# Layer 3's gathered matmuls of a four-layer graph-attention stack, given as two column halves each

## The chip, the cores and the metric

The kernel runs on one core of a Trainium2 chip. A core has TensorE (matmuls, shown as PE, with its weight loads as PEld), VectorE (DVE), ScalarE (ACT), GpSimd (POOL), SyncE (SP, which only issues transfers here) and 16 DMA engines. The metric is the device time of one execution in microseconds; lower is better.

## The reference

Four graph-attention layers over 4096 nodes of 256 features, each followed by a residual sum and a layer norm. The adjacency is the same in every layer: an edge with probability 1/256, and the diagonal. Layer 3, cut to what matters:

```python
h = x @ W                                    # 4096 x 256
Wh1, Wh2 = h @ a[:256], h @ a[256:]
e = leaky_relu(Wh1 + Wh2.T, 0.2)             # 4096 x 4096
att = softmax(where(adj > 0, e, -1e12), axis=1)
neg = -softmax(where(adj > 0, -e, -1e12), axis=1)
out = elu(concatenate([att @ x, neg @ x], axis=1) @ fc_W)
x = layernorm(x + out)
```

Layers 0 and 1 have four heads of 64 features, layer 2 two heads of 128. Layer 3 has two "heads" of 256, the positive and the negative softmax. Everything is float32.

## The kernel before

**Tiles.** The 4096 destination nodes are 32 row tiles of 128. A row tile has edges to only some of the source nodes, so its sources are packed: 13 lists of 128 source nodes, gathered by index from HBM, and the tile's own 128 nodes make 14 positions of 128 nodes (`NP` = 14), handled as two halves of 7 (`HALF`). At each position the values `G` hold, for every source node, 257 columns per head in layer 3: 256 values that were multiplied by the softmax's source factor, and one column that collects the denominator. The values are the projected ones, that is, already multiplied by `fc_W`.

**One half tile in layer 3** (`RowTile.half`, `n == 3`). ACT forms the scores for 7 positions (L690) and two exponentials over all of them (L691, L693); DVE masks both (L692, L694). That gives weights `w[1]` and `w[0]`, each 128 source nodes x 7 positions x 128 destination nodes. TensorE then runs, for head 1 and then head 0, seven matmuls that add into that head's own accumulator, `accs[1]` or `accs[0]`, each one PSUM bank (L727). The weights `w[h][:, k, :]` are the stationary operand (128 rows by 128 columns), and the 257 columns of `G` stream past. `start` is given at position 0 and `stop` at position 13. The very last half tile is done position by position (`last_half`, matmuls at L741). In layer 2 the same line adds both heads into one bank, with 129 columns each; in layers 0 and 1 the operands are swapped (L724).

**Whole rows.** Four of the 32 row tiles of layer 3 (one block, `WHOLE[3] = (7,)`) aren't packed: `whole_rows` runs all 32 source tiles for them, dense, from plain transfers, with matmuls of 128 x 128 weights and 257 streamed columns (L1027). These units are dealt out between the half tiles of the other 28 row tiles by `Layer.whole`: after most half tiles comes one unit of four matmuls.

**Order.** Each engine runs its instructions in the order in which the program gives them (`half_with_whole`): matmuls of a half tile, then the previous tile's finish (`positive`, L1099 and L1102, and `finish`, L1119 to L1127, which read the accumulators), then a unit of the whole rows. POOL issues the gathers for the tiles to come (L647), into 30 buffers that come free as the matmuls that read them end. The accumulators of layer 3 rotate through two pools, for even and odd half-tile steps of a tile's start. SP carries masks, edge terms and plain value tiles.

**Other shapes of TensorE's work** that the prediction speaks of: L278 (layer weights folded with the attention vectors; 128 x 128 weights, 1 to 4 streamed columns), L287 (layer 2's bias term; one column of weights), L557 and L560 (projection; L560 adds a bias with one row of weights), L589 (transposes of 1 to 4 columns) and L757 (transposes of 65 rows).

Of the kernel before, what the change touches and what calls it, by code (L numbers as in the profile page):

```python
# [50 lines left out]
P = 128  # L51
# [22 lines left out]
HALF = NP // 2  # L74
# [531 lines left out]
class RowTile:  # L606
# [25 lines left out]
    def load(self, half):  # L632
        L, m, n = self.layer, self.m, self.layer.n
        prog, nc, sh = L.prog, L.nc, L.shared
        if half == 0:
            self.S = prog.ld.tile([P, H4, P], F32, name="S")
            nc.sync.dma_start(out=self.S[:, :TERMS[n]], in_=sh["e"][n][m].partition_broadcast(P))
            self.mk = prog.ld.tile([P, NP, MC], U8, name="mk")
            nc.sync.dma_start(out=self.mk, in_=sh["maskC"][m])
        else:  # L640
            self.y = L.load_x(m)
        for pos in range(HALF * half, HALF * (half + 1)):
            if pos == FRONT:
                nc.sync.dma_start(out=self.place(pos), in_=sh["v"][n][m * P:(m + 1) * P, :])
                continue
            t = pos - (pos > FRONT)
            nc.gpsimd.indirect_dma_start(  # L647
                out=self.place(pos), out_offset=None, in_=sh["v"][n][:NODES[t], :],
                in_offset=bass.IndirectOffsetOnAxis(ap=sh["idx"][:, m, pos:pos + 1], axis=0))

    def half(self, half):
        L, n, nc = self.layer, self.layer.n, self.layer.nc
        prog, sh, S = L.prog, L.shared, self.S
        H, Wd, V, T, A = HEADS[n], WIDTH[n], VALS[n], TERMS[n], LOGS[n]
        if self.accs is None:
            pool = prog.ptwo[1 if n == 3 and self.step % 2 else 0]
            self.accs = [prog.bank(pool) for _ in range(2 if n == 3 else 1)]
        accs = self.accs
        G = [self.place(half * HALF + k) for k in range(HALF)]
        mh = self.mk[:, half * HALF:(half + 1) * HALF, :]  # L660
        if n < 2:

            if prog.masks is None:
                prog.masks = prog.bank(prog.pmask)
            there = prog.masks[:, half * BANK // 2:half * BANK // 2 + HALF * P // 4].bitcast(I32)
            nc.vector.tensor_scalar(there.rearrange("p (t i) -> p t i", t=HALF),
                                    mh.rearrange("p t i -> p (t i)").bitcast(I32)
                                    .rearrange("p (t i) -> p t i", t=HALF)[:, :, :P // 4], 0, None,
                                    op0=ALU.bitwise_or)
            mh = there.bitcast(U8)  # L670
            mh2 = mh.rearrange("p (o i) -> p o i", o=1).to_broadcast([P, 2, HALF * P])
        else:
            mh = mh[:, :, :P]
        pairs = [prog.wp.tile([P, 2, HALF, P], F32, name="w") for _ in range(H // 2)]
        w = [pair[:, k] for pair in pairs for k in range(2)]
        if n < 2:
            w = [w[1], w[2], w[3], w[0]]
        def masked(pair):

            pair = pair.rearrange("p h t i -> p h (t i)")  # L680
            nc.vector.scalar_tensor_tensor(pair, pair, LEAST, mh2, op0=ALU.max, op1=ALU.mult)  # L681

        def d(k, h):
            return G[k][:, V + T + h:V + T + h + 1]

        if n == 3:
            if half == 1 and self.step == L.count - 1:
                return self.last_half(accs, G, w, mh)
            for k in range(HALF):
                nc.scalar.activation(w[0][:, k, :], S[:, 0, :], AF.Relu, bias=d(k, 0))  # L690
            nc.scalar.activation(w[1], w[0], AF.Exp, scale=-1.0)  # L691
            nc.vector.tensor_tensor(w[1], w[1], mh, op=ALU.mult)  # L692
            self.exps = nc.scalar.activation(w[0], w[0], AF.Exp, bias=sh["shift2"])  # L693
            nc.vector.tensor_tensor(w[0], w[0], mh, op=ALU.mult)  # L694
            heads = (1, 0)
        else:
            for h in range(A, T):
                k = 0
                while k < HALF:
                    pos = half * HALF + k  # L700
                    e = 2 if pos % 2 == 0 and k + 1 < HALF else 1
                    if e == 2:
                        dd = self.slots[pos // 2][:, :2 * ROW[n]].rearrange("p (t c) -> p t c", t=2)
                        nc.vector.tensor_tensor(  # L704
                            w[h][:, k:k + 2, :], S[:, h:h + 1, :].to_broadcast([P, 2, P]),
                            dd[:, :, V + T + h:V + T + h + 1].to_broadcast([P, 2, P]), op=ALU.mult)
                    else:
                        nc.vector.tensor_scalar(w[h][:, k, :], S[:, h, :], d(k, h), None, op0=ALU.mult)
                    k += e
            for h in range(A):  # L710
                for k in range(HALF):
                    nc.scalar.activation(w[h][:, k, :], S[:, h, :], AF.Exp, bias=d(k, h))  # L712
                if n == 2:
                    nc.vector.scalar_tensor_tensor(w[h], w[h], LEAST, mh, op0=ALU.max, op1=ALU.mult)  # L714
                elif h % 2 == 0:
                    masked(pairs[h // 2])
            heads = list(range(A, H)) + list(range(A))
        for h in heads:
            for k in range(HALF):
                pos = half * HALF + k  # L720
                how = dict(start=pos == 0 and (n == 3 or h == heads[0]), stop=pos == NP - 1, skip_group_check=True)
                v = G[k][:, h * Wd:(h + 1) * Wd]
                if n < 2:
                    nc.tensor.matmul(accs[0][:Wd, h * P:(h + 1) * P], v, w[h][:, k, :], **how)  # L724
                else:
                    a = accs[h][:, :Wd] if n == 3 else accs[0][:, h * Wd:(h + 1) * Wd]
                    nc.tensor.matmul(a, w[h][:, k, :], v, **how)  # L727

    def last_half(self, accs, G, w, mh):

        nc, sh, Wd = self.layer.nc, self.layer.shared, WIDTH[3]
        V, T = VALS[3], TERMS[3]
        for k in range(HALF):
            d = G[k][:, V + T:V + T + 1]
            nc.scalar.activation(w[0][:, k, :], self.S[:, 0, :], AF.Relu, bias=d)
            nc.scalar.activation(w[1][:, k, :], w[0][:, k, :], AF.Exp, scale=-1.0)
            nc.vector.tensor_tensor(w[1][:, k, :], w[1][:, k, :], mh[:, k, :], op=ALU.mult)
            nc.scalar.activation(w[0][:, k, :], w[0][:, k, :], AF.Exp, bias=sh["shift2"])
            nc.vector.tensor_tensor(w[0][:, k, :], w[0][:, k, :], mh[:, k, :], op=ALU.mult)
            for h in (1, 0):  # L740
                nc.tensor.matmul(accs[h][:, :Wd], w[h][:, k, :], G[k][:, h * Wd:(h + 1) * Wd],  # L741
                                 start=False, stop=k == HALF - 1, skip_group_check=True)

    def copy(self):

# [19 lines left out]
class Layer:  # L765
# [26 lines left out]
    def load(self, m, half):  # L792
        if m < self.count and (m, half) not in self.loaded:
            self.loaded.add((m, half))
            self.tile(m).load(half)
# [794 lines left out]
```

## Time and profile before

| | us |
|---|---|
| median of 3 runs | 2253.98 |
| lowest and highest run | 2251.62, 2256.02 |
| span of the profiled execution | 2249.3 |
| TensorE matmul busy in it | 2014.0 (90%) |
| TensorE weight load busy | 1834.3 (82%) |
| DVE, ACT, POOL busy | 1786.6 (79%), 1737.9 (77%), 1494.4 (66%) |
| mean granted TensorE clock | 0.966 |
| layer 3's matmuls, first to last | 1757 to 2232 |

The page gives the profiled execution's own time by its span, from the first to the last instruction; the median lies 4.7 us above that span. A group's line gives its source line, engine, operation, what it writes and reads, shapes and count; then busy us and mean ns of one, and the idle time before it with what ended it. Matmuls are pipelined, and one is shown from its start until its result is out, so neighbours overlap: the distance between two starts, not the shown length, is what a matmul costs. A float32 matmul of the program appears as two passes, each with a weight load (LDWEIGHTS) and a matmul. A timeline line gives the start and the length of a run of equal instructions, and their number. The chain of work that ended last follows, back from the last instruction, what each step waited for.

### The profile page before, as it was taken

To read this page: it belongs to the slowest core of one execution; us is meant where nothing else is said; L and a number is where in the kernel's file an instruction comes from. 1 tells how busy PE (TensorE), PEld (TensorE's weight loads), DVE (VectorE), ACT (ScalarE), POOL (GpSimd) and SP (SyncE) were. 2 spreads that over 40 slices of the span, in tenths; PEclk is the share of its full clock that TensorE was granted. 3 is DMA by queue.
4 is the path that set the end of the run, shared out by engine and by line. 5 is a ranking of instruction groups with operands and counts; after the bars stand their busy time and mean duration, and the time that the engine had idled before them with its cause. 6 is when DMAs were issued, how large, how long until landed. Compare 5 with 4: busy or idle time off the path is not lost. (4 is left out here: it accounts for less than half of the span.)

```text
span 2249.3 us, 49137 instructions
## 1 busy us (share of the span) xinstructions
PE 2014.0 (90%) x15689; PEld 1834.3 (82%) x15689; DVE 1786.6 (79%) x5060; ACT 1737.9 (77%) x4989; POOL 1494.4 (66%) x1597
## 2 busy tenths in 40 slices
PE   4878889989999969988899898989999999999995
PEld 2658788878899859988888798989998888788784
DVE  2889899999999959987988886887876566566566
ACT  4778988988789859987888776987876677667664
POOL 2107655656677777777777777777773477777773
PEclk7999999999999989999999999999999999999998
DMA  8879877777566665666665666777777688888884
GB/s 284 258 245 360 272 219 250 254 247 228 146 170 191 174 202 168 182 175 175 173 185 162 172 167 171 226 209 223 223 227 225 200 282 280 249 284 270 262 248 130
DMA packets 250319, 492.99 MB, mean 219 GB/s; under 512 B 44385, under 2 KB 156610, under 8 KB 249666
## 3 DMA queue, kind: packets, MB, share of 16 engines
q0 software_dynamic: 81536, 245.30, 38.3%
q1 hardware_dynamic: 163906, 240.26, 33.3%
q10 hardware_dynamic: 4608, 4.20, 0.5%
q8 instruction: 126, 2.06, 0.4%
q14 instruction: 143, 1.17, 0.2%
HBM read 437.05 MB, written 52.54 MB: 218 GB/s over the span
## 5 line engine op out<-in xcount | busy, mean ns | idle before, releaser
L647 POOL DMA_INDIRECT G<-vals,idx x1456 | 1480.7, 1017 | 715.7 <-issue 221.1
L712 ACT ACTIVATE w<-S,G 128x128 f32<-128x128 f32 x3248 | 1001.6, 390 | 140.6 <-DMA G<-vals,idx 101.6
L724 PE MATMUL bank<-w,G 128*65 128x128 f32 x7168 | 837.8, 276 | 59.7 <-DVE w L681 59.3
L724 PEld LDWEIGHTS bank<-w,G 128*65 128x65 f32 x7168 | 798.7, 140 | 69.9 <-DVE w L681 68.4
L681 DVE SCALAR_TENSOR_TENSOR w<-w,bank 128x1792 f32<-128x1792 f32 x256 | 514.6, 2013 | 13.4 <-ACT w L712 11.2
L727 PE MATMUL bank<-G,w 128*128 128x257 f32 (+1 forms) x2660 | 490.8, 342 | 25.7 <-ACT z L1102 13.6
L727 PEld LDWEIGHTS bank<-G,w 128*128 128x128 f32 x2660 | 431.9, 195 | 73.2 <-ACT z L1102 16.4
L1027 PE MATMUL bank<-vw,pw 128*128 128x129 f32 (+1 forms) x2048 | 298.5, 301 | 3.7 <-issue 2.3
L1027 PEld LDWEIGHTS bank<-vw,pw 128*128 128x128 f32 x2048 | 273.6, 191 | 20.1 <-issue 2.8
L690 ACT ACTIVATE w<-S,G 128x128 f32<-128x128 f32 x385 | 137.8, 393 | 136.8 <-DMA G<-vals,idx 90.0
L440 DVE TENSOR_SCALAR oh<-iota,place 128x256 bf16<-128x256 f16 (+2 forms) x992 | 221.8, 298 | 9.4 <-PE bank L446 9.1
L704 DVE TENSOR_TENSOR w<-S,G 128x256 f32<-128x256 f32 x384 | 151.9, 416 | 69.9 <-DMA G<-vals,idx 66.5
L446 PE MATMUL bank<-mk,oh 128*128 128x132 fp8e4 x2336 | 192.1, 226 | 13.8 <-ACT cm L453 7.0
L557 PE MATMUL bank<-wext,xT 128*128 128x268 f32 (+3 forms) x640 | 176.9, 409 | 16.9 <-ACT xT L548 14.1
L446 PEld LDWEIGHTS <-oh 128*128 128x128 bf16 x2336 | 146.9, 99 | 50.4 <-DVE oh L440 12.7
L385 ACT ACTIVATE mk<-raw 128x1024 uint8<-128x1024 int32 x128 | 130.5, 1051 | 28.0 <-DMA raw<-in_adjB_dram 27.7
L557 PEld LDWEIGHTS bank<-wext,xT 128*128 128x128 f32 x640 | 117.2, 200 | 36.0 <-ACT xT L548 16.9
L1017 DVE SCALAR_TENSOR_TENSOR pw<-pw,mw 128x512 f32<-128x512 f32 x192 | 127.6, 689 | 18.2 <-ACT pw L1016 17.5
L1016 ACT ACTIVATE pw<-Sw,d 128x512 f32<-128x512 f32 x192 | 133.2, 711 | 7.5 <-PE bank L1027 7.0
L714 DVE SCALAR_TENSOR_TENSOR w<-w,mk 128x896 f32<-128x896 f32 x80 | 86.6, 1086 | 41.1 <-ACT w L712 37.9
L1024 DVE TENSOR_TENSOR pw<-pw,mw 128x512 f32<-128x512 f32 x64 | 43.6, 691 | 85.4 <-ACT pw L1023 48.0
L692 DVE TENSOR_TENSOR w<-w,mk 128x896 f32<-128x896 f32 x55 | 60.0, 1091 | 59.5 <-ACT w L691 58.2
(140 smaller groups left out, 1563.3 us busy)
## 6 DMA issues: line engine op xcount, KB each, us to landing
raw<-in_adjB_dram SPq DMA_DIRECT2D x128, 512.0 KB
mk<-maskC SPq DMA_DIRECT2D x112, 231.0 KB
G<-vals,idx POOLq DMA_INDIRECT x1456
S<-edge SPq DMA_DIRECT2D x64, 256.0 KB
vw<-vals SPq DMA_DIRECT2D x96, 129.0 KB
xp<-y SPq DMA_DIRECT2D x96, 128.0 KB
y<-xp SPq DMA_DIRECT2D x96, 128.0 KB
mw<-maskW SPq DMA_DIRECT2D x20, 528.0 KB
```

What stands on the lines that cost most here:

```text
L440: nc.vector.tensor_scalar(oh[:, :n * P], iota[:, :n * P], self.place[:, it, j:j + 1], None, op0=ALU.is_equal)
L446: nc.tensor.matmul(accs[b][:, s * MC:(s + 1) * MC], oh[:, (k - a) * P:(k - a + 1) * P], mk[:, j, it, :].bitcast(FP8), start=touches[b][0] ...
L557: nc.tensor.matmul(pp[:, :c1 - c0], self.xT[:, k, :], wext[:, k, c0:c1], start=(k == 0), stop=(k == KT - 1 and brow is None))
L647: nc.gpsimd.indirect_dma_start(out=self.place(pos), out_offset=None, in_=sh["v"][n][:NODES[t], :], in_offset=bass.IndirectOffsetOnAxis(ap= ...
L681: nc.vector.scalar_tensor_tensor(pair, pair, LEAST, mh2, op0=ALU.max, op1=ALU.mult)
L690: nc.scalar.activation(w[0][:, k, :], S[:, 0, :], AF.Relu, bias=d(k, 0))
L704: nc.vector.tensor_tensor(w[h][:, k:k + 2, :], S[:, h:h + 1, :].to_broadcast([P, 2, P]), dd[:, :, V + T + h:V + T + h + 1].to_broadcast([P ...
L712: nc.scalar.activation(w[h][:, k, :], S[:, h, :], AF.Exp, bias=d(k, h))
L724: nc.tensor.matmul(accs[0][:Wd, h * P:(h + 1) * P], v, w[h][:, k, :], **how)
L727: nc.tensor.matmul(a, w[h][:, k, :], v, **how)
L1016: nc.scalar.activation(p, S[:, h], AF.Exp, bias=d)
L1027: nc.tensor.matmul(accs[it][:, c:c + Wd], p[:, it, :], v[:, c:c + Wd], start=(j == 0 and h == heads[0]), stop=(j == NT - 1), skip_group_ch ...
```

## The change

In layer 3 each gathered matmul is given as two. The first takes the weights of the upper 64 destination nodes and writes accumulator rows 0 to 63, the second those of the lower 64 and rows 64 to 127. Both stream the same 257 columns of `G`. Each thus uses 64 of the array's 128 columns: the first the lower-numbered half, the second the other. `start` and `stop` are given to both. The same is done in `last_half`. Layer 2's matmuls and the whole rows stay as they were.

```diff
                 if n < 2:
                     nc.tensor.matmul(accs[0][:Wd, h * P:(h + 1) * P], v, w[h][:, k, :], **how)
+                elif n == 2:
+                    nc.tensor.matmul(accs[0][:, h * Wd:(h + 1) * Wd], w[h][:, k, :], v, **how)
                 else:
-                    a = accs[h][:, :Wd] if n == 3 else accs[0][:, h * Wd:(h + 1) * Wd]
-                    nc.tensor.matmul(a, w[h][:, k, :], v, **how)
+                    for r in (slice(0, P // 2), slice(P // 2, P)):
+                        nc.tensor.matmul(accs[h][r, :Wd], w[h][:, k, r], v, **how)
...
             for h in (1, 0):
-                nc.tensor.matmul(accs[h][:, :Wd], w[h][:, k, :], G[k][:, h * Wd:(h + 1) * Wd],
-                                 start=False, stop=k == HALF - 1, skip_group_check=True)
+                for r in (slice(0, P // 2), slice(P // 2, P)):
+                    nc.tensor.matmul(accs[h][r, :Wd], w[h][:, k, r], G[k][:, h * Wd:(h + 1) * Wd],
+                                     start=False, stop=k == HALF - 1, skip_group_check=True)
```

## The prediction

> **What bounds the kernel now.** I read the page first (parts 1, 2, 5), then the chain of work that ended last, piece by piece, for layer 3, then the stretches in which TensorE idles, and last the few places where the kernel already leaves the full array.
>
> ```profile
> PE 2014.0 (90%) x15689; PEld 1834.3 (82%) x15689; DVE 1786.6 (79%) x5060; ACT 1737.9 (77%) x4989; POOL 1494.4 (66%) x1597
> PE   4878889989999969988899898989999999999995
> PEclk7999999999999989999999999999999999999998
> ```
>
> TensorE is the busiest engine, fullest in the last quarter. Layer 3's matmuls run from 1757 to 2232 us. Its groups, and the chain there:
>
> ```profile
> L727 PE MATMUL bank<-G,w 128*128 128x257 f32 x1429 | 326.6, 387 | 18.2 <-ACT z L1102 13.6 <-DVE w L692 4.7
> L727 PEld LDWEIGHTS bank<-G,w 128*128 128x128 f32 x1428 | 276.2, 194 | 61.6 <-ACT z L1102 16.4 <-DVE w L692 5.1
> L647 POOL DMA_INDIRECT G<-vals,idx x316 | 324.4, 1026 | 96.3 <-PE bank L727 31.4 <-issue 27.1 <-DMA G<-vals,idx 19.2
> ```
>
> ```profile
> 1774.95 6.07 PE bank L727 x28
> 1781.01 3.47 PE bank L1027 x16
> 1784.48 6.07 PE bank L727 x28
> ```
>
> One f32 matmul of the program is two in the trace, each with its own weight load. A half tile has 7 positions x 2 heads = 14 matmuls, 28 passes; 6.07/28 = 0.2167 us per pass, although a pass is shown 0.39 long (pipelined) and its weight load 0.19. So the load lies wholly beside the previous pass, and what counts is the 257 columns that stream past: the pass itself is the bound. Layer 3's gathered work is 28 tiles x 14 positions x 2 heads = 784 matmuls = 1568 passes = 339.8 us; the whole rows (L1027) are 512 passes = 110.9 us. Together 450.7 of the 475 us. TensorE's reserve is in four stretches:
>
> ```profile
> 1934.00:1948.00 14.00, 8.44 (x24) 5.91 (x24) 10.05 (x34) 12.47 (x32) 10.95 (x11) 0.76 0.84 249
> 2064.00:2101.00 37.00, 34.62 (x159) 29.72 (x158) 22.89 (x67) 24.94 (x54) 28.47 (x29) 1.00 0.85 266
> 2101.00:2126.00 25.00, 21.50 (x86) 18.01 (x85) 16.08 (x49) 16.80 (x35) 19.51 (x19) 0.86 0.81 239
> 2197.00:2222.00 25.00, 17.48 (x70) 14.38 (x69) 20.16 (x76) 18.04 (x46) 17.39 (x18) 0.86 0.74 214
> ```
>
> Columns are the stretch, its length, busy PE, PEld, DVE, ACT, POOL, the granted clock. PE idles 5.6 + 2.4 + 3.5 + 7.5 = 19 us and loses some 10 more to the lower clock after an idle gap. These 29 us are all that a slower TensorE could swallow. Who waits for whom in layer 3 (us in total, times, longest):
>
> ```profile
> ACT w L690 <- DMA G<-vals,idx: 75.8, 79, 6.8
> POOL G L647 <- PE bank L727: 40.8, 111, 7.2
> ```
>
> ACT waits for gathered data, and POOL's gathers wait for buffers that L727 frees; neither is late enough to stop TensorE outside the four stretches.
>
> **The change, part by part.** 784 matmuls become 1568; in the trace 1568 passes and 1568 loads are added. A half has 64 columns of weights but streams the same 257 columns, so nothing in a pass becomes shorter by what is known here. Given one after the other, the halves need twice the time; given at once in two halves of the array, the old time. There is no gain in sight, since the old pass already used every column of the array. No DMA, ACT, DVE or POOL instruction is added or moved.
>
> First unknown, **do the halves stream at once?** The order for one position is upper pass 1, upper pass 2, lower pass 1, lower pass 2. Best case: upper pass 2 runs beside lower pass 1, and lower pass 2 beside the next position's upper pass 1, 0.433 per position as now. Worst case: four passes one after the other, +0.433 x 784 = +339.8 us. No row of this trace has two different tiles of the array at work, so both ends stay.
>
> Second unknown, **the load at each change of half.** In the trace no load ever starts before the matmul ahead of it in the program has started: loads and matmuls strictly alternate, x15689 each. With that order, lower pass 1's load starts when upper pass 2 starts, and lower pass 1 waits for it; so does the next upper pass 1. The price of an exposed load has two rows:
>
> ```profile
> 821.07 0.14 PEld L287 LDWEIGHTS bank<-ablk,bcol 128*1 128x1 f32 x4
> 821.24 0.97 PEld L278 LDWEIGHTS bank<-ablk,nat 128*128 128x128 f32 x8
> 2100.13 0.48 PE L727 MATMUL bank<-G,w 128*128 128x257 f32 x1 [1.32 <-ACT z L1102]
> ```
>
> Eight loads that nothing hides: (0.97 - 0.19)/7 = 0.11 us for 128 columns; and the first pass after an idle gap is shown 0.48 long against 0.38. For 64 columns I take half, 0.055; ends 0 (loaded further ahead) and 0.11. Two changes per position: 784 x 2 x 0.055 = 86 us (0 to 172). I take 86, as the strict alternation is the only row on the order.
>
> The Trainium skill speaks against the change here: "TensorE: Matmul & The Clock Gate" (Part 3, The mechanism) says that a load overlaps a running matmul only where the row groups differ, and both halves use all rows. This trace contradicts it for one full-array tile, where the load starts with the running matmul. Taken literally it would expose all four loads of a position, 784 x 4 x 0.055 = +172 us; the same section's measured stagger of about 4 ns between packed matmuls would make it only 784 x 2 x 0.004 = +6 us.
>
> Third, **the change between array shapes.** Whole rows keep 128 columns, so the PE queue now switches twice per burst; layer 3 has 51 gathered bursts. L287 (one column of weights) and L560 (one row) are the places where the kernel already leaves the full shape:
>
> ```profile
> 820.64 0.41 PEld L278 LDWEIGHTS bank<-ablk,nat 128*128 128x128 f32 x3
> 1048.53 0.70 PE L560 MATMUL bank<-brow,ones 1*128 1x262 f32 x2
> 1049.16 0.26 PEld L757 LDWEIGHTS bank<-ident,aT 65*128 65x128 f32 x3 [0.34 <-issue]
> ```
>
> The third L278 load starts at 820.86 and is through at 820.97; L287's starts at 821.07, 0.10 later, though it waits for nothing. On the way back, L287's fourth matmul starts at about 821.14 (25 ns apart) and the next load at 821.24, 0.10 again. L560 to L757: 1049.16 - 1048.53 = 0.63 for two passes of 0.218, so 0.19 over: 0.11 of exposed load and 0.08 to 0.09 of emptying. L589, also few columns, shows no such gap; but it is a transpose, not a matmul as here. I take L287: in, 0.10 + 0.055; out, 0.10 + 0.11. 51 x 0.155 + 50 x 0.21 = 18.4 us (bounds 0, by L589, and that). Queued behind it are the L1027 matmuls and, through the buffers that they and L727 free, POOL's gathers and ACT's z.
>
> Fourth, **the end of a burst.** The last lower pass has no partner: 51 x (0.217 - 0.055) = 8.3 us (0 if serial, 11.1 if loads are hidden).
>
> Sum: 86 + 18.4 + 8.3 = 113 us. Of the reserve I take off 20 of 29: the idle stretches come from late work on ACT and DVE (ACT waits 75.8 us for gathered data in layer 3), which gains time when TensorE slows; the hand-over of an accumulator through z stays. Net +93. The profiled execution spans 2249.3; the median of the timed runs, 2253.98, lies 4.7 above it, and that margin is kept: 2249.3 + 93 + 4.7 = 2347 us.
>
> **The rivals.**
> *Serial halves:* 339.8 + 18.4 - 25 of reserve = +333, 2587 us. For it: nothing in the trace ever shows two matmuls in parallel. Against: the two halves share no columns and no accumulator rows.
> *Fully parallel, loads ahead of time:* 18.4 + 11.1 plus a stagger of 0 to 0.025 us per change (the closest matmul starts on record, L287), 0 to 39; less 10 of reserve. +19 to +58; I take +25, 2279 us. Against: the strict alternation above.
> *Faster:* the half shape streams its columns quicker than 0.217 per pass. It decides once a position takes under 0.433 - 29.5/784 = 0.396 us. At half the time, 170 us would be freed, but POOL's gathers hold: of its idle time in layer 3 only 41 us wait for L727, so about 2254 - 41 = 2213 us. Against: every f32 row, 128 or 257 columns long, streams at the same rate. For it: no row shows a 64-column tile. The skill's "TensorEngine Tiling (Array Packing)" (Theoretical Speedup) promises up to 2x where a dimension is at most 64, which by itself would lead here; but it compares with an array that stands half empty, and this one is full.
> *No change:* parallel, no emptying (as L589), the reserve swallowing 11.1 us of burst ends: 2254 us.
>
> **How the numbers follow.** Exposed loads 0.35 (the likeliest, 2347), fully parallel 0.27, serial 0.27, faster 0.07, no change 0.04. The range goes from 2264 (parallel with more of the reserve) to 2600 (serial with little of it): it leaves out the last two cases and the edges, under 0.2. The likeliest case alone spans 2300 (load half as dear) to 2440 (0.11 per load, all reserve kept). A difference of 0.2% (4.5 us) is about what can be told from no change: faster 0.07, same 0.04, slower 0.89.
>
> **What the changed profile would show.** The burst in the chain tells it: 56 passes in about 6.6 us if parallel, 14 x 0.544 + 0.16 = 7.8 if loads are exposed, 12.1 if serial, 6.07 or less if I am wrong in sign. The switch shows as a gap of some 0.15 to 0.2 us between L1027's passes and the gathered ones on either side; the four idle stretches shrink; POOL waits longer for the gathered matmuls than 40.8 us; the 128-column passes stay at 0.217. The prediction fails most of all if different column halves do, or don't, overlap for f32, which no row here decides.

## The result

The changed kernel takes 2260.17 us (median of 18 runs) against 2252.96 (18 runs); the ratio is 1.003 with a 95% interval of 1.0019 to 1.004, that is 4.3 to 9.0 us slower. The sign was forecast, the size was not: 2347 was predicted, with 2264 as the low end.

From the page of the changed kernel, parts 1, 2 and 5 (the gathered line is now L729, the whole rows L1030, ACT's z L1105):

```profile
PE 2031.3 (90%) x17257; PEld 1759.3 (78%) x17257; DVE 1787.1 (79%) x5060; ACT 1737.3 (77%) x4989; POOL 1495.5 (66%) x1597
PE   4878889989999969989889898999998999999996
PEclk7999999999999979999999998999999999999998
L729 PE MATMUL bank<-G,w 128*64 128x257 f32 x3080 | 351.8, 387 | 9.1 <-ACT z L1105 4.9
L729 PEld LDWEIGHTS bank<-G,w 128*64 128x64 f32 x3080 | 219.3, 139 | 135.2 <-issue 14.8
```

There are twice as many gathered passes (3080 and 56 at the last half tile, against 1568), but their busy time is what it was: 351.8 us here, and 350.9 in the same stretch before. So two passes run side by side. The chain of waits shows it burst by burst, first the changed kernel, then a line of the kernel before, then who waits for whom in the changed kernel:

```profile
1777.15 6.22 PE bank L729 x56
1783.37 3.67 PE bank L1030 x16
1787.03 6.22 PE bank L729 x56
1803.13 1.93 PE bank L1030 x8
```

```profile
1800.08 1.73 PE bank L1027 x8
```

```profile
POOL G L647 <- PE bank L729: 24.8, 54, 8.3
```

56 half passes take 6.22 us; the 28 whole ones took 6.07. Eight whole-row passes take 1.93 instead of 1.73, sixteen 3.67 instead of 3.47. So bursts of either kind became 0.15 to 0.2 us longer; of the 50 gathered bursts of 56 passes, 49 take 6.22 us. POOL's gathers wait less for the gathered matmuls than before (24.8 against 40.8 us), not more as I had written.

Where the 0.15 and 0.2 us lie is seen in the weight loads. TensorE's load timeline, the changed kernel and then the kernel before (start, length, then in brackets the idle time ahead):

```profile
1785.36 1.27 PEld L1030 LDWEIGHTS bank<-vw,pw 128*128 128x128 f32 x6
1786.96 5.83 PEld L729 LDWEIGHTS bank<-G,w 128*64 128x64 f32 x56 [0.33 <-issue]
1793.18 1.38 PEld L1030 LDWEIGHTS bank<-vw,pw 128*128 128x128 f32 x7 [0.39 <-issue]
```

```profile
1783.45 0.62 PEld L1027 LDWEIGHTS bank<-vw,pw 128*128 128x128 f32 x3
1784.10 6.04 PEld L727 LDWEIGHTS bank<-G,w 128*128 128x128 f32 x28
1790.17 1.92 PEld L1027 LDWEIGHTS bank<-vw,pw 128*128 128x128 f32 x9
```

Before, loads follow one another; now an idle 0.33 and 0.39 us stands at the two changes of shape, put down to "issue", a wait for nothing that the profile names. The starts of the matmuls around one such burst, taken from the same trace (us, and distance to the one ahead):

```
1786.654  whole row, last pass
1786.964  half pass   +0.310
1786.970  half pass   +0.006
1787.231  half pass   +0.261
1787.238  half pass   +0.007
1787.448  half pass   +0.210
1787.454  half pass   +0.006
   (and so on, in pairs, 0.217 from pair to pair)
1792.864  half pass   +0.210
1792.871  half pass   +0.007
1793.181  whole row   +0.310
1793.502  whole row   +0.321
1793.719  whole row   +0.217
```

A pass normally starts 0.217 after its predecessor. Going in, the first pair starts 0.310 after the last whole pass and the second pair 0.267 after the first: (0.310 - 0.217) + (0.267 - 0.217) = 0.143 us. I read the first part as the array emptying and the second as a 64-column load that nothing hides. Coming out costs 0.093 plus 0.104, for a 128-column load, 0.197 us. Layer 3 has 51 ways in and 50 out: 17.1 us.

It doesn't all reach the time. The table splits layer 3's stretch, from the first to the last pass of 257 columns, into 2080 pass times of 0.2167 us (a pair counted once), changes of shape at the prices above, idle gaps over 0.6 us, and a rest (mostly passes at half clock after a gap). Each column is from that kernel's own trace, all on chips where the kernel before takes about 2253.

```
                       before  after    e2     e3     e4    e5d
first to last pass      488.5  492.5  495.7  497.7  495.8  591.7
passes                  450.7  450.7  450.7  450.7  450.7  450.7
changes of shape, in        0     51      0    111     56    381
changes of shape, us        0   17.1      0   37.5   18.8  129.3
idle gaps over 0.6 us    28.0   17.8   34.1    8.6   21.6    8.6
rest                      9.8    6.9   10.9    0.9    4.7    3.1
```

In the changed kernel, 10 us of idle gaps and 3 us of the rest are gone: 17.1 - 13.1 = 4.0 us in layer 3. The other 1.6 us of the two spans' difference (2254.9 against 2249.3) lies ahead of layer 3, where nothing was changed. Each column is a single execution, though, and executions of one kernel differ by more than that: those of the kernel before took 2247.77 to 2260.53 us, and e2, without a change of shape, has 6 us more of idle gaps than the kernel before. So the size of the loss rests on the 18 runs, the price of a change of shape on the bursts, and the 4.0 us is the account of this one pair of traces. The stretches around two of the gaps, after (columns as in the prediction):

```profile
1944.00:1956.00 12.00, 7.80 (x41) 4.50 (x41) 9.21 (x28) 11.13 (x30) 9.25 (x10) 0.72 0.88 264
2203.00:2225.00 22.00, 17.08 (x138) 10.20 (x136) 19.11 (x71) 15.23 (x38) 17.43 (x16) 0.92 0.71 197
```

TensorE idles 4.2 and 4.9 us there; of the four stretches shown before, the ones near 2064 and 2101 no longer have a gap.

### The profile page after: what moved, and what is told of

Read it like the earlier page. It is cut to its first block, busy times and chain, and to the rows that moved or that the text cites. A ratio compares the mean times of both kernels' runs of the same rounds, so it can differ in the third digit from the quotient of the medians.

```text
span 2254.9 us, 52275 instructions
## 1 busy us (share of the span) xinstructions
PE 2031.3 (90%) x17257; PEld 1759.3 (78%) x17257; DVE 1787.1 (79%) x5060; ACT 1737.3 (77%) x4989; POOL 1495.5 (66%) x1597
## 5 line engine op out<-in xcount | busy, mean ns | idle before, releaser
L724 PE MATMUL bank<-w,G 128*65 128x128 f32 x7168 | 841.9, 277 | 54.0 <-DVE w L681 53.7
L724 PEld LDWEIGHTS bank<-w,G 128*65 128x65 f32 x7168 | 803.6, 141 | 63.4 <-DVE w L681 61.9
L729 PE MATMUL bank<-G,w 128*64 128x257 f32 x3080 | 351.8, 387 | 9.1 <-ACT z L1105 4.9
L729 PEld LDWEIGHTS bank<-G,w 128*64 128x64 f32 x3080 | 219.3, 139 | 135.2 <-issue 14.8
L1030 PE MATMUL bank<-vw,pw 128*128 128x129 f32 (+1 forms) x2048 | 303.5, 304 | 2.4 <-issue 1.8
L1030 PEld LDWEIGHTS bank<-vw,pw 128*128 128x128 f32 x2048 | 269.8, 192 | 34.5 <-issue 20.1
L726 PE MATMUL bank<-G,w 128*128 128x129 f32 x1120 | 140.2, 283 | 6.4 <-DVE w L714 6.4
L1020 DVE SCALAR_TENSOR_TENSOR pw<-pw,mw 128x512 f32<-128x512 f32 x192 | 127.6, 690 | 17.9 <-ACT pw L1019 17.1
L726 PEld LDWEIGHTS bank<-G,w 128*128 128x128 f32 x1120 | 135.3, 199 | 7.1 <-DVE w L714 6.6
```

The lines of the kernel that those rows point to most:

```text
L726: nc.tensor.matmul(accs[0][:, h * Wd:(h + 1) * Wd], w[h][:, k, :], v, **how)
L729: nc.tensor.matmul(accs[h][r, :Wd], w[h][:, k, r], v, **how)
L1030: nc.tensor.matmul(accs[it][:, c:c + Wd], p[:, it, :], v[:, c:c + Wd], start=(j == 0 and h == heads[0]), stop=(j == NT - 1), skip_group_ch ...
```

## The experiments

The runs fell on several chips. The kernel before takes 2252 to 2254 us on the chips of e1 to e4 and of e5d and e6d, and 2753 to 2791 on those of e5, e5b, e5c, e6, e6b, e6c, e7, e8, a2 and b2, so ratios are given only against the kernel before on the same chip. Each of these chips ran at one time only, so what is said here of a chip may belong to the time as well.

My theory after the result was A: halves stream at once, and only the changes of shape cost. The rival, B: the loss comes with the number of half matmuls (instructions, two streams of the same data).

**e1: all upper halves first.** How does TensorE find a partner for a pass? The program gives a position as upper pass 1, upper pass 2, lower pass 1, lower pass 2. If passes started strictly in that order, a burst would begin and end with a lone pass, 29 pass times; it takes 28. So lower pass 1 must have started ahead of upper pass 2, and what I had written of the engines' order, that each follows the program, doesn't hold for TensorE's passes. e1 puts 14 upper passes ahead of the first lower one.

```diff
-        for h in heads:
-            for k in range(HALF):
...
-                    for r in (slice(0, P // 2), slice(P // 2, P)):
+            for h in heads:
+                for r in (slice(0, P // 2), slice(P // 2, P)):
+                    for k in range(HALF):
```

> The same 1568 half matmuls, but per head all seven upper halves first and then all seven lower ones: 14 passes of one half stand in the queue ahead of the first pass of the other. Theory A (TensorE starts a pass of the other half ahead of earlier ones that still wait, as far back as its queue reaches): if the reach is at least 28 instructions, a burst stays at about 6.2 us and the time within 0.3% of the changed kernel's, 2260. Theory B (it only reaches the next few instructions): each half streams alone, a burst goes to 28 x 0.217 x 2 = 12.1 us, and the time to about 2254 + 340 + 17 - 25 = 2586. In between: overlap only where one head's lower half meets the next head's upper half, a burst of about 9 us, 2420.

Measured: 2433.41 us, ratio 1.0791 (1.0749 to 1.0833). Its chain, and then passes of the gathered line in successive stretches of one burst (length, TensorE busy with the passes that it holds, loads, clock, share of the transfer engines, GB/s; a pass that reaches into a stretch is counted there too):

```profile
1786.09 9.85 PE bank L723 x56
1795.93 3.67 PE bank L1038 x16
```

```profile
1799.50:1801.70 2.20, 2.17 (x10) 1.42 (x11) 1.00 0.84 284
1801.70:1802.60 0.90, 0.90 (x9) 0.72 (x8) 1.00 0.94 298
1802.60:1803.95 1.35, 1.35 (x9) 0.82 (x6) 1.00 0.72 203
1803.95:1804.80 0.85, 0.85 (x9) 0.70 (x8) 1.00 0.88 238
```

It is the case in between: ten passes alone in 2.2 us, then eight new ones in 0.9 (four pairs), six alone in 1.35, again four pairs. The first lower pass starts together with the eleventh upper one, while three upper passes still wait. (The records don't name a pass's half, but its first pass is shown 0.431 us long instead of 0.380, and the one beside the eleventh is.) So a pass starts ahead of at most three waiting passes of the other half. By that rule four pairs form at each of the burst's three joints, which makes 56 - 12 = 44 pass times; at each joint the half that starts anew trails by a load of about 0.056 us, 0.17 us in all. The burst of 9.85 us, less 0.15 for the change of shape, is 44.8 times 0.2167: the 44 and these three loads. (The 45 in the expectation of e8 below is one too many.) Had passes kept strictly to the program's order, only the last upper pass would have met a lower one at each joint, 53 pass times or 11.6 us.

**e8: groups of three and four positions**, a forecast by that rule.

```diff
-            for h in heads:
-                for r in (slice(0, P // 2), slice(P // 2, P)):
-                    for k in range(HALF):
+            for h, ks, r in ((h, ks, r) for h in heads for ks in (range(3), range(3, HALF))
+                             for r in (slice(0, P // 2), slice(P // 2, P))):
+                for k in ks:
```

> Per head and half tile: upper halves of positions 0 to 2, lower halves of 0 to 2, upper of 3 to 6, lower of 3 to 6. The upper-then-lower run's bursts of 9.85 us fit a rule that a pass may start ahead of at most three waiting passes of the other half: 45 pass times by that rule, 44.7 measured. Theory A (that rule): 33 pass times of 0.2167 us and 0.15 for the change of shape, a burst of 7.3 us (6.6 to 7.5). Reach of two: 8.4; of one: 9.9. Theory B (only the order by position lets halves overlap, by chance of their waits): 9 us or more.

```profile
2238.72 7.25 PE bank L724 x56
2245.97 3.67 PE bank L1039 x16
```

The chain has bursts of 7.25 us; 7.3 was expected for a reach of three, 8.4 for two. Counted as above, a reach of three gives 32 pass times and three loads, 7.25 us; a reach of two 35 pass times, about 7.9, and one of four 31, about 7.0. Of the 50 bursts of 56 passes 30 take 7.25 us; the others have gaps in them, as on the other chips of this kind (below). The single run took 2786.79 us against 2753.59; the forecast was of the burst alone.

**e2: the whole rows in halves too**, which leaves layer 3 without a change of shape inside.

```diff
-                            nc.tensor.matmul(accs[it][:, c:c + Wd], p[:, it, :], v[:, c:c + Wd],
+                            for r in (slice(0, P // 2), slice(P // 2, P)) if n == 3 else (slice(0, P),):
+                                nc.tensor.matmul(accs[it][r, c:c + Wd], p[:, it, r], v[:, c:c + Wd],
```

> Layer 3's whole rows are given in halves as well, so that layer 3 has no change of array shape but its first and last. Theory A (the loss is the change of shape, 0.14 us in and 0.20 us out, 51 times): the 17 us go, bursts are 28 x 0.217 = 6.07 us again, time equal to before within 0.2%, 2250 to 2257. Theory B (the loss is the number of instructions or the two streams' reads of the same data): 1024 more passes and loads, so another third to two thirds of the loss on top: 2262 to 2266.

Measured: 2256.87 against 2254.26, ratio 1.0015 (0.9998 to 1.0031). All 2080 pass times are pairs, and no change of shape is left in the trace. The idle gaps are back at 34.1 us. That is against B, which wanted 2262 to 2266, although 1024 more passes and loads were added; it agrees with A, but the interval reaches from no loss to that of the changed kernel, so by itself it proves little.

**e3 and e4: more changes, or fewer half matmuls.** e3 gives the first four positions of a head in halves and the last three whole; e4 only head 1 in halves.

```diff
-                    for r in (slice(0, P // 2), slice(P // 2, P)):
+                    for r in (slice(0, P // 2), slice(P // 2, P)) if k < 4 else (slice(0, P),):
```

```diff
-                    for r in (slice(0, P // 2), slice(P // 2, P)):
+                    for r in (slice(0, P // 2), slice(P // 2, P)) if h == 1 else (slice(0, P),):
```

> Per head and half tile the first four positions are given in halves, the last three whole: two changes into and two out of the half shape per half tile, 112 of each instead of 51 and 50. Theory A: 112 x 0.34 = 38 us of switches against 17 us in the changed kernel, so 21 us more less what idle time takes up, 2268 to 2282. Theory B (cost per half matmul, of which there are 4/7): the loss of 7 us shrinks to 4, about 2257.

> Only head 1's matmuls are given in halves, head 0's whole: half as many half matmuls (last half tile aside), about as many changes of shape (55 into, 55 out). Theory A (cost per change of shape): the same loss as in the changed kernel, 2258 to 2263. Theory B (cost per half matmul): half the loss, about 2257.

Measured: e3 2260.81, ratio 1.0021 (1.0002 to 1.004); e4 2258.08, ratio 1.0019 (1.0001 to 1.0038). The time can't tell A from B in either, and e3 misses my 2268. The table shows why: e3's 37.5 us of changes have taken up every idle gap in the middle of the layer (8.6 us are left; 8.0 to 8.6 us of gaps stand in the layer's first 11 us in each of the table's kernels) and nearly all of the rest, the half clock after them. Doubling a cost that is smaller than the reserve it falls into shows nothing.

**e5: a cost well above the reserve.** Positions alternate, halves and whole: 392 changes each way by the program, 381 and 380 in layer 3's recorded passes.

```diff
-                    for r in (slice(0, P // 2), slice(P // 2, P)):
+                    for r in (slice(0, P // 2), slice(P // 2, P)) if k % 2 == 0 else (slice(0, P),):
```

> Positions 0, 2, 4, 6 of each head and half tile are given in halves, positions 1, 3, 5 whole: seven changes into the half shape and seven out per half tile, 392 each. Theory A (cost per change of shape: 0.143 us in, 0.197 us out): 133 us against 17 in the changed kernel; idle time in layer 3 can take up at most 29, so 2358 us and not under 2345. Theory B (cost per half matmul, 4/7 as many): about 2257.

> Positions 0, 2, 4, 6 of each head and half tile in halves, positions 1, 3, 5 whole, beside a kernel before of about 2254. Theory A (0.34 us per pair of changes of shape, 392 pairs): layer 3's matmuls take 451 us of passes, 133 us of changes and only the 9 us of idle time that stand at the layer's start; against 488 in the profile before, 104 us longer: 2345 to 2365. Theory B (cost per half matmul, 4/7 as many as in the changed kernel): about 2257.

> As before for this kernel: 133 us of changes of shape in layer 3. On a chip like the first, 2345 to 2365 against 2254 (theory A) or 2257 (theory B). On a chip where the queue runs dry: +45 to +55 us over before as already seen there, and the gaps in layer 3's passes of the kernel before make up the rest, some 50 us of them.

> The alternating kernel on whichever chip it gets. Where the kernel before takes about 2254: layer 3 at 451 + 133 + 9 = 593 us against 488, 2345 to 2365 in all (theory A), or 2257 (theory B). Where it takes about 2750 to 2790: +1.5 to 1.8%, as seen.

Measured where the kernel before takes 2252.3 (e5d): 2352.32, ratio 1.045 (1.0423 to 1.0476), +100 us. A said +104, B +3 to 5. Who waited for whom, e5d:

```profile
PEld bank L729 <- issue: 211.2, 589, 0.4
```

The same wait is 14.8 us in the changed kernel. In the table, e5d's stretch is accounted for to 3 us with the prices read from the changed kernel's trace. This settles the cost where the kernel before takes about 2253: it goes with the changes of shape, not with the half matmuls.

On the other chips the same kernel gave ratios of 1.0172 (1.0128 to 1.0217), 1.0183 (1.0131 to 1.0235) and 1.015 (1.0108 to 1.0192): 43 to 51 us. Two runs beside e5c say where the rest went, the unchanged kernel before (b2) and the unchanged changed kernel (a2).

> The kernel before, unchanged, for a trace from the same chip as the three runs beside it. On a chip like that of the first profiles: 2254, layer 3's passes over 489 us with 28 us of idle gaps over 0.6 us. On a chip like those of the alternating runs: about 2753, and then the question is how long its layer 3 is. Theory A (only changes of shape cost in layer 3): near 490 plus whatever gaps of about 0.7 us TensorE's queue shows there; Theory B (layer 3 of the alternating kernel was long because of the chip): near 550 or more.

> The changed kernel beside the same chip's traces. On a chip like the first: 2258 to 2262. On a chip where TensorE's queue runs dry now and then: the same 17 us of changes of shape, and twice the gathered instructions of layer 3 to fetch; between 0 and 30 us above before.

b2: 2792.12 (one run). On this chip TensorE's work has holes, waits that nothing in the profile explains; who waited for whom, b2:

```profile
PE bank L724 <- issue: 215.6, 280, 3.2
PE bank L727 <- issue: 50.8, 64, 5.2
PE bank L1027 <- issue: 41.3, 45, 2.4
```

The first of these lines has no counterpart among the waits of the first profile, and other engines show the like: POOL's gathers wait 396.7 us for "issue", 221.1 in the first profile. Counted in the traces, 295 distances between neighbouring matmul starts lie between 0.55 and 0.8 us in b2, 33 in the first profile of the same program. Layer 3 takes 549.3 us there, with 76.5 in idle gaps, instead of 488.5 with 28.0. In e5c, 592.8 us, only 9.2 of gaps are left: the holes close while the changes of shape hold TensorE back, and 592.8 - 549.3 = 43.5 us is the whole difference of the times (2834.64 - 2791.43 = 43.2). The changed kernel (a2) is 1.0106 (1.0066 to 1.0147) of before there; its layer 3 takes 575.9 us, 27 more than b2's, and 25 of its 50 bursts take 7.0 us or more instead of 6.22, where b2 has 16 of 50 that take as much. Of the 27 us, 17.1 are changes of shape at the prices above. Whether the other 10 are a cost of the doubled instructions there, or the scatter of single executions (2781.54 to 2803.35 us for the kernel before), isn't shown; nor is what makes the holes.

**e6 and e7: is a half worth having where loads bind?** In the changed kernel the two 64-column loads start 6 ns apart, so 128 columns of weights are in after about 0.055 us instead of 0.11. In layers 0 and 1 that would allow the operands to be swapped, so that only 65 columns stream and the transposes back aren't needed. e6 does so in halves, e7 with whole loads; layer 3 is as in the kernel before.

```diff
                 if n < 2:
-                    nc.tensor.matmul(accs[0][:Wd, h * P:(h + 1) * P], v, w[h][:, k, :], **how)
+                    for r in (slice(0, P // 2), slice(P // 2, P)):
+                        nc.tensor.matmul(accs[0][r, h * Wd:(h + 1) * Wd], w[h][:, k, r], v, **how)
...
     def copy(self):
-        L = self.layer
...
+        return
     def back(self):
-        L = self.layer
...
+        return
```

> From the kernel before, with layer 3 whole. In layers 0 and 1 the operands are swapped: the weights of 128 destination nodes are loaded, in two halves, and the 65 columns of the values stream; the transposes back and the copy ahead of them go. What the changed kernel showed of the two halves (loads and passes start 6 ns apart and run side by side) would make a position and head, now two passes of 109 ns, two pairs of passes, each pair bound by 65 columns (about 57 ns) or by the 64-column load (about 55 ns). Theory A (loads of two halves run side by side): 3584 matmuls x 2 x (109 - 57) = 370 us less of TensorE in layers 0 and 1, where it is busy 86 to 93% beside DVE and ACT at 80 to 95%: 2170 to 2235 us. Theory B (loads share one path, 107 ns per pair): TensorE's time as before, less the transposes; 2240 to 2260.

> As the kernel with swapped operands in layers 0 and 1, but with whole 128-column loads: the control. A pass is bound by its 128-column load, about 110 ns by L278, as long as now; the transposes and their copies go. Theory A: 2240 to 2260, and the difference to the halved form is what parallel loads bring. Theory B: the same as the halved form.

> Layers 0 and 1 with swapped operands and 64-column halves, layer 3 as in the kernel before, beside a kernel before of about 2254. Theory A (loads of the two halves run side by side, so a pair of passes takes about 57 ns instead of 109, and TensorE's shorter time is not lost elsewhere): 2170 to 2235 us. Theory B (TensorE with shorter bursts and gaps is granted the half clock more often, and changes of shape beside the packing matmuls cost 0.34 us each): no gain, 2254 or more.

> Layers 0 and 1 with swapped operands in 64-column halves. On a chip like the first: 2170 to 2235 if shorter bursts on TensorE come through, 2254 or more if half clock and changes of shape eat them. On a chip where the queue runs dry: +11 to 12%, as already seen.

> Layers 0 and 1 with swapped operands in halves. Where the kernel before takes about 2254: 2170 to 2235 if the shorter bursts come through; 2254 or more if twice the instructions, the half clock and the changes of shape eat them. Where it takes about 2750 to 2790: +11 to 12%, as seen.

Measured where the kernel before takes 2252.3 (e6d): 2251.44, ratio 0.9999 (0.9983 to 1.0014). Its gathered line and DVE's masking in layers 0 and 1, from the page:

```profile
L725 PE MATMUL bank<-G,w 128*64 128x65 f32 x14336 | 560.4, 247 | 237.2 <-DVE w L681 230.0
L725 PEld LDWEIGHTS bank<-G,w 128*64 128x64 f32 x14336 | 526.7, 160 | 297.0 <-DVE w L681 261.9
L681 DVE SCALAR_TENSOR_TENSOR w<-w,bank 128x1792 f32<-128x1792 f32 x256 | 515.4, 2016 | 37.7 <-ACT w L712 36.0
```

```profile
L724 PE MATMUL bank<-w,G 128*65 128x128 f32 x7168 | 837.8, 276 | 59.7 <-DVE w L681 59.3
```

The last line is the kernel before, 837.8 us of TensorE. The most common burst of e6d, one head pair, takes 1.63 us for 28 pairs of passes, 0.058 from pair to pair, where 28 passes took 3.00. So TensorE does get through nearly twice as fast, against the rival that loads share one path. But it then waits 230 us for DVE's masked weights, where it had waited 59.3, and the gathered matmuls of layers 0 and 1 end only 13 us earlier (1326 against 1339 us). Layer 2, whose work is unchanged, starts as much earlier and ends 2 us later than before (1743.3 against 1741.5); what takes the 13 us back there, the runs don't tell. So TensorE wasn't what set the end of layers 0 and 1. Its mean granted clock is lower, too, 0.905 against 0.966. On the other chips e6 takes 1.1133 (1.1086 to 1.118), 1.1173 (1.1119 to 1.1228) and 1.1177 (1.1136 to 1.1219) of before, and e7, beside the first of these, 1.1746 (1.1688 to 1.1804) at a mean clock of 0.691 against e6's 0.797. The halved form beats the whole one there by 179 us, of which the runs can't tell the shorter loads from the higher clock, but neither beats the kernel before, and no version tried does.

## Why the prediction was right and wrong

- *What bounds layer 3* was right: the passes stream at 0.2167 us, in halves too, and the added costs fell on TensorE's own path.
- *"Do the halves stream at once?"* I took the best case as the likeliest, and it holds: 0.2167 per pair.
- *"The load at each change of half", 86 us: this is the step that failed.* The term is zero. I read the strict alternation of loads and matmuls in the trace of before as an order that TensorE keeps. What the runs show instead: a load still starts 2 ns after a pass (1787.233 after 1787.231), but only one of its own half; the other half's load and pass don't wait for it, and passes are taken ahead of up to three waiting ones (e1, e8). So 28 pairs take 28 pass times, with no load exposed inside a burst. That the alternation before was forced by a single tile being in use is my reading of this. The trace of before couldn't have shown it, and I should have given the end "loaded further ahead" more weight than the middle.
- The Trainium skill, "TensorE: Matmul & The Clock Gate" (Part 3, The mechanism), was the other way to price that step. Its rule that loads overlap a running matmul only across row groups doesn't hold here: two halves share all rows, and their loads overlap each other and the passes. A few lines above that rule the section also lets a load be pulled ahead into a background weight buffer, an exception that I left out; read with it, the page doesn't say that the loads are exposed. The stagger that it gives, about 4 ns, was near: 6 to 7 ns are measured. It is not even lost, since the second of a pair ends as much later as it started. The same list says that matmuls start strictly in order; e1's burst of 44.8 pass times instead of 53 contradicts it for two column halves.
- *"The change between array shapes", 18.4 us,* was right: 17.1 measured, from L287's and L560's rows, and e5d confirms the price 129 us large. Taking L287 rather than the transpose L589 as the nearest row was the right choice. "TensorEngine Tiling (Array Packing)" (Key Properties) says that a change of tiling mode drains the engine; the traces agree, with 0.093 us to empty and 0.05 or 0.10 for the exposed load.
- *"The end of a burst", 8.3 us,* is zero as well (7 ns): partners are found from the first pass to the last.
- *The reserve:* I took off 20 of 29 us. Idle gaps and rest gave up 13 of 37.8 in the changed kernel's trace; a larger cost takes more (e3: 28; e5d: 26).
- The sum with the failed terms put right is 17.1 - 13.1 = +4.0 us by that one pair of traces, beside a measured +4.3 to +9.0. The rival *fully parallel* (2279) was the right mechanism, but also carried 11.1 us of burst ends and a stagger, of which the bursts show nothing, and I gave it only 10 us of reserve; with the measured 17.1 and 13.1 in their place it is 2254 + 4 = 2258. So even the low end of my range, drawn from that rival, missed by 4 us. *Serial* and *faster* are refuted: a pair takes 0.2167 us, neither twice that nor less. (The dear end that I gave for the likeliest case, 2440, should by its own terms have been about 2450.)

## What to carry to other kernels

Column halves of TensorE run side by side, for float32 too, if a pass has no more than three waiting passes of the other half ahead of it in the program; they bring nothing where whole passes already stream without a break, and each trip into another array shape and back cost 0.34 us here. Halves do make loads overlap, which may be worth trying where 128-column loads bind and TensorE sets the end of the stage; no run here gained by it. And to test a small cost, make it larger than the idle time it falls into: doubling it was invisible here, multiplying it by eight was clear to 4 us.

## What the runs showed of the hardware that I had not expected

- Passes of one column half start ahead of up to three waiting passes of the other (e1: a burst of 44.8 pass times where strict order gives 53; e8: 7.25 us, as the rule gives).
- Two 64-column weight loads run side by side: 28 pairs of passes with 65 streamed columns take 1.63 us, 0.058 us from pair to pair, where one exposed 128-column load takes 0.11.
- The mean granted clock was lower in the kernel whose TensorE waits more: 0.905 in e6d, which idles 237 us ahead of its gathered line in layers 0 and 1, against 0.966 and 60 us before, at the same time.
- The same program takes 2253 us on some chips and 2753 to 2791 on others, where TensorE waits 215.6 us ahead of L724 alone for nothing that the profile shows; the cause stays open.
